# A selective scan on one core: GpSimd takes a coming tile's inputs ahead of two of its three products with C, and the sums over those products come one to two slots later

## The chip, the cores and the metric

The kernel runs on one core of a Trainium2 chip. The core's engines work side by side, each through its own queue in order: TensorE (PE in the profile, its weight loads PEld), VectorE (DVE), ScalarE (ACT), GpSimd (POOL) and SyncE (SP), which here issues all DMA transfers. They wait for each other through semaphores. The metric is the device time of one execution in microseconds.

## The reference, cut to what matters

A VSS-style block (layer norm, depthwise convolution, a selective scan in four directions, a gated norm, two convolutions with a channel gate) is followed by attention without softmax and a quantized feed-forward. The scan takes nearly all of the time:

```python
def _selective_scan(u, delta, A, Bs, Cs, D):      # 8 images, 4 directions, 192 channels, 4096 positions
    ...
    def step(hst, inp):
        u_i, dt_i, b_i, c_i = inp
        dA = jnp.exp(dt_i[..., None] * A)          # 16 states for each channel
        hst = dA * hst + (dt_i * u_i)[..., None] * b_i[:, :, None, :]
        y = jnp.einsum('bkdn,bkn->bkd', hst, c_i)
        return (hst, y)
    ...
    _, ys = lax.scan(step, h0, (u_t, dt_t, b_t, c_t))
    return ys.transpose(1, 2, 3, 0) + D[None, :, :, None] * u
```

## The kernel before, in words

The scan is cut into 256 *units*: 8 images, 4 directions (`order` 0 to 3) and 8 chunks of 512 positions. A unit has 192 channels times 16 states, that is 24 rows of work of 128 partitions by 512 positions. They are the 24 *slots* of a unit, in six tiles of four (`TILES`, `G` = 4): tile n has slots 4n to 4n + 3. Tiles 0 to 2 use the first half of B and C, tiles 3 to 5 the second.

What is done for one slot:

- ScalarE makes the decay, `da` = exp(delta * A) (L1111), into one of three PSUM banks, two slots ahead.
- GpSimd has made the inputs of the whole tile, `hb` = B * du, 128x2048, in `inputs` (L990). There are six `hb` buffers, so that a tile takes the buffer of the same tile of the unit before.
- VectorE scans (L1177). In a *banked* slot (`BANKED`: all of tiles 0, 2 and 4, and one or two slots of tile 5) the states go back into the PSUM bank and VectorE then multiplies them with C (L1179), and ScalarE copies the last state to `carry` (L1180) before the bank is used again. In the other slots the states go to `hb`, and ScalarE copies the carry of the whole tile once (L1185) after its last scan.
- For the slots that are not banked GpSimd multiplies with C, one instruction for a tile, in `outputs` (L996). A unit has three of these *lots*: tile 1 and tile 3 (128x2048) and what is left of tile 5 (128x1024 or 128x1536). It must follow the carry's copy, since it overwrites the states.
- TensorE adds up the states by products with a 0/1 matrix, in `sums` (L1016), in PSUM: tiles 0 and 1 together, tile 2, tiles 3 and 4 together, tile 5. After tile 5 it adds D * u or the sum so far (L1025), and ScalarE copies the result out in two pieces, `yt` (`gather`, L1035 in the transposed directions, L1038 in the others), which SP writes to HBM.

Beside it run the step sizes of the coming units (`step_sizes`: TensorE L955, ScalarE L963, L965 and L967, VectorE L969, GpSimd L972), their spread over partitions by DMA (`spread`, L984), the loads of B and C (`states`, L924), and two streams of *side work*: the front of the next image and the back end of the last one. A stream goes on by itself, a few instructions a slot: it issues a matmul group and its eviction (on ScalarE or VectorE) two slots later. `gated`, the first stage of the back end, takes a chunk once its y has been gathered.

The order of all queues is written out by hand. `plan` lists what is issued after the scan of each of the unit's 24 slots, and the main loop at the end of the function runs through the units and slots: first the carry copies left from the slot before, then the `da` of two slots on, the scan, its product with C, then the plan's list for the slot in the order in which it was put, then the side work. Each engine's queue is in that order; nothing is reordered afterwards. So what is put at an earlier slot stands further ahead in its engine's queue, and everything behind an instruction that waits, waits too.

Of the kernel before, what the change touches and what calls it, by code (L numbers as in the profile page):

```python
# [43 lines left out]
def kernel(ctx: ExitStack, tc: tile.TileContext, a, out):  # L44
# [689 lines left out]
    for b in range(out.shape[0]):  # L734
# [3 lines left out]
        for order, (pair, back) in enumerate((p, k) for p in s["pairs"] for k in range(2)):  # L738
            for i in range(NC):
                u = Unit()  # L740
# [305 lines left out]
    def plan(u, last, nxt, third):  # L1046

        at = [[] for _ in range(24)]

        def put(slot, f, *args):  # L1050
            at[slot].append((f, args))

        if last:
            put(0, outputs, last, 5)
            put(0, before, last)
            for m in range(2):
                put(m, sums, last, (3, 4), 2 + m)
            for m in range(2):
                put(5 + m, sums, last, (5,), m)
            put(7, states, u, 1, 1)  # L1060
            put(10, gather, last, 0)
            put(11, gather, last, 1)
        for n in range(6):
            to = (u, n + 2) if n < 4 else (nxt, n - 4)
            if to[0]:
                put(4 * n + 1, inputs, *to)
        if third and u.i % 2:
            put(16, step_sizes, (nxt, third), 5)
        put(8, outputs, u, 1)
        put(16, outputs, u, 3)  # L1070
        for m in range(4):
            put(13 + m, sums, u, (0, 1), m)
            if m < 2:
                put(18 + m, sums, u, (2,), m)
                put(22 + m, sums, u, (3, 4), m)
        if nxt:
            for i, slot in enumerate((0, 2, 4)):
                put(slot, step_sizes, (nxt,), i + 3)
            put(4, spread, nxt, 0, (0, 1))
            put(6, spread, nxt, 1, (0, 1))  # L1080
            put(10, states, nxt, 0, 0)
            put(15, states, nxt, 1, 0)
            put(20, states, nxt, 0, 1)
            if u.i % 2 == 0:
                put(15, spread, nxt, 0, (2,))
                put(16, spread, nxt, 1, (2,))
        if third:
            put(1, fetched_dt, third)
            put(9, fetched_u, third)
            for i, slot in enumerate((20, 22, 23)):  # L1090
                put(slot, step_sizes, (third,), i)
            if u.i % 2:
                for i, slot in enumerate((9, 11, 12, 13, 15)):
                    put(slot, step_sizes, (nxt, third), i)
                put(17, spread, nxt, 0, (2,))
                put(18, spread, nxt, 1, (2,))
            elif u.i + 3 < len(units):
                put(21, fetched_pair, third, units[u.i + 3])
        return at

    def at_index(i):
        return units[i] if 0 <= i < len(units) else None
# [39 lines left out]
    for u in units:  # L1142
        last, nxt, third = (at_index(u.i + d) for d in (-1, 1, 2))
# [19 lines left out]
        if u.start:  # L1163
            carry = sp.tile([P, 24], F32, tag="carry", name="carry")
        todo = plan(u, last, nxt, third)
        for slot in range(24):
            n, m = divmod(slot, G)
# [112 lines left out]
```

## Time and profile before

| | |
|---|---|
| runs | 11,218.44, 11,230.6 and 11,228.5 us; median 11,228.5 |
| profiled execution | 11,232.69 us, its span 11,230.9 us |
| scan loop, first scan to end of the last | 243.4 to 10,991.9 us |
| instructions of L1177, L996, L990 | 6,144, 768, 1,536 |
| mean of one, L1177 | 1.20 to 1.28 us by form |
| mean of one, L1179 | 0.69 us |
| one of L990 | 4.54 us |
| one of L996 | 4.53 us (128x2048), 3.45 (128x1536), 2.37 (128x1024) |
| one of L972, L1111, L1038 | 1.28, 0.69, 0.58 us |
| granted TensorE clock | 0.82 of full speed, mean |

Each line of the profile's groups gives a line of the kernel, the engine, what is written and read, the shape and the count; then the busy time in us and the mean of one in ns; and behind the bar the time that the engine sat idle just before these instructions, with what ended most of it. In the lists of waits a line reads: who waited, for whom, us in total, times, and the longest. In an order of time, the first two columns are the start and the duration in us, and brackets give the idle time before and its releaser.

### The profile page before, as it was taken

The page shows a single profiled execution, that of the slowest core. Times are in us where ns is not written, and L with a number is a line of the kernel's source. Part 1 is how long each engine was busy: PE and PEld are TensorE (multiplying, and loading weights), DVE is VectorE, ACT ScalarE, POOL GpSimd, SP SyncE. Part 2 cuts the span into 40 slices and gives each one's busy share as a digit, 9 for nine tenths or more (in the row PEclk, how much of TensorE's full clock was granted, in tenths as well). Part 3 has the DMA queues.
Part 4 walks back from the last instruction along what each step waited for, and adds up shares of the span by engine and source line. Part 5 has one row for each costly group of instructions (what it writes and reads, how often), then busy time and mean ns, then how long its engine had stood idle before and what let it go on. Part 6 is the DMA issues. An engine that isn't in the chain of part 4 may idle for free. (4 is left out here: it accounts for less than half of the span.)

```text
span 11230.9 us, 97011 instructions
## 1 busy us (share of the span) xinstructions
PE 8540.9 (76%) x23270; PEld 2316.7 (21%) x23270; DVE 10389.6 (93%) x10870; ACT 7480.8 (67%) x14898; POOL 10398.6 (93%) x2782
## 2 busy tenths in 40 slices
PE   7767668887788877887678876888767887676677
PEld 2111112221122211222112221222212221111212
DVE  1999999999999999999999999999999999999993
ACT  3666666667666676667766676676766667666674
POOL 1999999999999999999999999999999999999991
PEclk7887778887788877888788887888878888787778
DMA  4888888888888888888888888889888898888883
GB/s 108 203 194 206 190 196 211 213 219 199 200 211 217 207 197 213 204 216 214 192 215 205 215 218 196 203 210 226 202 202 212 208 223 199 193 196 199 201 200 91
DMA packets 1095376, 2253.25 MB, mean 201 GB/s; under 512 B 435993, under 2 KB 436698, under 8 KB 963731
## 3 DMA queue, kind: packets, MB, share of 16 engines
q1 hardware_dynamic: 1094803, 2247.05, 82.4%
q8 instruction: 184, 3.01, 0.1%
q14 instruction: 389, 3.19, 0.1%
HBM read 1507.14 MB, written 336.69 MB: 164 GB/s over the span
## 5 line engine op out<-in xcount | busy, mean ns | idle before, releaser
L990 POOL TENSOR_TENSOR hb<-b,du 128x2048 f32<-128x2048 f32 x1536 | 6938.9, 4535 | 9.0 <-PE p L1016 6.7
L1111 ACT ACTIVATE da<-delta,w_a_logs 128x512 f32<-128x512 f32 x6144 | 4216.9, 690 | 693.8 <-DVE hb L1177 573.0
L1016 PE MATMUL p<-hb,halves 128*64 128x512 f32 x12288 | 3813.7, 729 | 784.4 <-POOL hb L996 375.7
L1177 DVE TENSOR_TENSOR_SCAN da<-da,carry,hb 128x512 f32<-128x512 f32 x3087 | 3949.4, 1279 | 55.5 <-ACT da L1111 51.6
L996 POOL TENSOR_TENSOR hb<-hb,c 128x2048 f32<-128x2048 f32 (+2 forms) x768 | 2984.2, 3886 | 302.8 <-ACT carry L1185 250.2
L1177 DVE TENSOR_TENSOR_SCAN hb<-da,carry,hb 128x512 f32<-128x512 f32 x2289 | 2781.6, 1265 | 61.9 <-ACT da L1111 61.0
L1179 DVE TENSOR_TENSOR hb<-da,c 128x512 f32<-128x512 f32 x3528 | 2440.0, 692 | 155.5 <-DMA c<-xd 1.6
L1180 ACT COPY carry<-da 128x1 f32<-128x1 f32 x3528 | 554.9, 157 | 2335.1 <-DVE hb L1179 2325.2
L1016 PEld LDWEIGHTS p<-hb,halves 128*64 128x64 f32 x12288 | 913.0, 161 | 3512.6 <-issue 2112.9
L313 PE MATMUL conv<-f0im,taps 97*128 97x512 f32 (+1 forms) x2088 | 910.0, 669 | 92.2 <-ACT f0pre L369 52.1
L1177 DVE TENSOR_TENSOR_SCAN da<-da,hb 128x512 f32<-128x512 f32 x441 | 537.7, 1219 | 15.2 <-POOL hb L990 14.1
L972 POOL TENSOR_TENSOR ua<-nat,ua 128x512 f32<-128x512 f32 x256 | 327.4, 1279 | 228.6 <-DMA ub<-u 224.2
L955 PE MATMUL dt<-dts,dt_w 7*64 7x512 f32 (+1 forms) x1024 | 451.5, 661 | 12.7 <-DVE nat L969 10.9
L1025 PE MATMUL p<-u,ident 128*128 128x512 f32 x768 | 441.2, 703 | 4.3 <-DMA u<-y 3.9
L313 PEld LDWEIGHTS conv<-f0im,taps 97*128 97x128 f32 (+1 forms) x2088 | 255.6, 175 | 683.2 <-issue 527.6
L1177 DVE TENSOR_TENSOR_SCAN hb<-da,hb 128x512 f32<-128x512 f32 x327 | 377.8, 1203 | 4.9 <-ACT da L1111 4.9
L253 PE MATMUL ctr<-f1e,cen_c 96*96 96x512 f32 x402 | 229.4, 679 | 132.3 <-DVE f1e L648 93.8
L259 PE MATMUL var<-f1e,ones_c 96*96 96x512 f32 x350 | 207.9, 678 | 148.5 <-ACT f1e L256 135.4
L1185 ACT COPY carry<-hb 128x4 f32<-128x4 f32 (+2 forms) x768 | 147.0, 191 | 196.2 <-DVE hb L1177 183.8
L497 PE MATMUL cab<-f1im,cab_w 97*32 97x512 f32 x1044 | 267.2, 632 | 11.3 <-DMA f1im<-xld 7.6
L534 PE MATMUL cab<-f1m,cab_w 96*96 96x512 f32 x348 | 204.3, 714 | 93.3 <-ACT f1e L543 41.4
L967 ACT ACTIVATE nat<-nat,one 128x512 f32<-128x512 f32 x384 | 272.5, 710 | 0.1
(428 smaller groups left out, 7504.8 us busy)
## 6 DMA issues: line engine op xcount, KB each, us to landing
b<-xd SPq DMA_DIRECT2D x1024, 512.0 KB
c<-xd SPq DMA_DIRECT2D x1024, 512.0 KB
delta<-nat SPq DMA_DIRECT2D x1536, 128.0 KB
du<-ua SPq DMA_DIRECT2D x1024, 128.0 KB
y<-yt SPq DMA_DIRECT2D x512, 256.0 KB
u<-y SPq DMA_DIRECT2D x384, 256.0 KB
ua<-u SPq DMA_DIRECT2D x256, 256.0 KB
du<-ub SPq DMA_DIRECT2D x512, 128.0 KB
```

The lines of the kernel that those rows point to most:

```text
L313: nc.tensor.matmul(ps, taps[:, t, lo : lo + n], im[:, r0 + dy : r0 + dy + 8, dx : dx + HW], start=t == 0, stop=t == 8,)
L955: nc.tensor.matmul(ps, dt_w.rearrange("r j d -> r (j d)")[32 * w.k : 32 * w.k + R + 1, d], w.dts, start=True, stop=True)
L967: nc.scalar.activation(u.nat, u.nat, AF.Ln, bias=one)
L972: nc.gpsimd.tensor_tensor(x, u.nat, x, ALU.mult)
L990: nc.gpsimd.tensor_tensor(hb, u.bc[0, g], u.du[j].unsqueeze(1).to_broadcast([P, G, T]), ALU.mult)
L996: nc.gpsimd.tensor_tensor(hb, hb, u.bc[1, TILES[n][0]][:, lo:, :], ALU.mult)
L1016: nc.tensor.matmul(ps, halves, u.hb[n][:, i, :], start=TILES[n][0] == 0 and m == 0, stop=False, skip_group_check=True)
L1025: nc.tensor.matmul(ps, w, x, start=False, stop=True, skip_group_check=True)
L1111: nc.scalar.activation(da[q], u.delta[j], AF.Exp, scale=a_neg[:, u.k, j, g * G + m : g * G + m + 1])
L1177: nc.vector.tensor_tensor_scan(dd if banked else x, dd, x, 0.0 if u.start else col, ALU.mult, ALU.add)
L1179: nc.vector.tensor_tensor(hb[:, m, :], d, u.bc[1, g][:, m, :], ALU.mult)
L1180: kept.append(lambda col=col, d=d, at=first_at: nc.scalar.copy(col, d[:, at : at + 1]))
```

## The change

Within `plan`, three things move; every instruction stays.

- Inputs: before, the six `inputs` of a unit's list stood at slots 1, 5, 9, 13 (tiles 2 to 5 of this unit), 17 and 21 (tiles 0 and 1 of the next). Now tile 2's stands at slot 0 and tile 4's at slot 8.
- Products with C on GpSimd: that of the last unit's tile 5 goes from slot 0 to slot 1, that of tile 1 from slot 8 to slot 9. So each of the two now follows an input which it stood ahead of. The product of tile 3 stays at slot 16.
- Sums, and what hangs on them: over tiles 0 and 1 from slots 13 to 16 to slots 15 to 18, over tile 2 from 18 and 19 to 19 and 20, over the last unit's tile 5 (with L1025) from 5 and 6 to 7 and 8; `gather` from 10 and 11 to 11 and 12. Those over tiles 3 and 4 stay at 22, 23, 0 and 1.

```diff
         def put(slot, f, *args):
             at[slot].append((f, args))
 
+
+        for n, slot in enumerate((0, 5, 8, 13)):
+            put(slot, inputs, u, n + 2)
         if last:
-            put(0, outputs, last, 5)
+            put(1, outputs, last, 5)
             put(0, before, last)
             for m in range(2):
                 put(m, sums, last, (3, 4), 2 + m)
             for m in range(2):
-                put(5 + m, sums, last, (5,), m)
+                put(7 + m, sums, last, (5,), m)
             put(7, states, u, 1, 1)
-            put(10, gather, last, 0)
-            put(11, gather, last, 1)
-        for n in range(6):
-            to = (u, n + 2) if n < 4 else (nxt, n - 4)
-            if to[0]:
-                put(4 * n + 1, inputs, *to)
+            put(11, gather, last, 0)
+            put(12, gather, last, 1)
         if third and u.i % 2:
             put(16, step_sizes, (nxt, third), 5)
-        put(8, outputs, u, 1)
+        put(9, outputs, u, 1)
         put(16, outputs, u, 3)
+        if nxt:
+            put(17, inputs, nxt, 0)
+            put(21, inputs, nxt, 1)
         for m in range(4):
-            put(13 + m, sums, u, (0, 1), m)
+            put(15 + m, sums, u, (0, 1), m)
             if m < 2:
-                put(18 + m, sums, u, (2,), m)
+                put(19 + m, sums, u, (2,), m)
                 put(22 + m, sums, u, (3, 4), m)
```

## The prediction

> **What bounds the kernel now.** I read four views, in this order: the page's busy shares and groups, the waits of VectorE and GpSimd inside the scan loop (250 to 10990 us), then the order of time at two places.
>
> ```profile
> span 11230.9 us, 97011 instructions
> PE 8540.9 (76%) x23270; PEld 2316.7 (21%) x23270; DVE 10389.6 (93%) x10870; ACT 7480.8 (67%) x14898; POOL 10398.6 (93%) x2782
> DVE  1999999999999999999999999999999999999993
> ...
> L990 POOL TENSOR_TENSOR hb<-b,du 128x2048 f32<-128x2048 f32 x1536 | 6938.9, 4535 | 9.0 <-PE p L1016 6.7
> ...
> L996 POOL TENSOR_TENSOR hb<-hb,c 128x2048 f32<-128x2048 f32 (+2 forms) x768 | 2984.2, 3886 | 302.8 <-ACT carry L1185 250.2
> ```
>
> VectorE and GpSimd are both busy for 93%. The groups tell them apart only in part: GpSimd idles 303 us ahead of its products with C, mostly until ScalarE has copied the carry of the tile that VectorE just scanned. So which of the two waits for the other?
>
> ```profile
> DVE hb L1177 <- ACT da L1111: 65.8, 92, 3.0
> DVE da L1177 <- ACT da L1111: 51.6, 22, 5.8
> ...
> DVE da L1177 <- POOL hb L990: 6.5, 8, 1.9
> ```
>
> ```profile
> POOL hb L996 <- ACT carry L1185: 241.6, 207, 4.3
> ...
> POOL hb L990 <- PE p L1016: 6.7, 9, 1.0
> ```
>
> GpSimd waits for VectorE for 241.6 us, VectorE for GpSimd for 6.5 us. VectorE sets the pace. All its waits over 150 ns in the loop come to 273 us (212 for ScalarE, 54 for TensorE, 6.5 for GpSimd); the other idle time is some 43 ns between each scan and its product (152 us in 3,528). Hence the change can win at most 273 us, and only where it makes ScalarE's `da` or an eviction come earlier; GpSimd's own 242 us are worth nothing by themselves.
>
> The 273 us recur in the same slot of the same unit of each image. The largest (32.2 us in six images) is slot 11 of an image's unit 6:
>
> ```profile
> 1813.46 3.39 PE L1016 MATMUL p<-hb,halves 128*64 128x512 f32 x8
> 1814.32 4.51 POOL L996 TENSOR_TENSOR hb<-hb,c 128x2048 f32<-128x2048 f32 x1 [4.26 <-ACT carry L1185]
> ...
> 1818.83 1.96 PE L253 MATMUL ctr<-f1e,cen_c 96*96 96x512 f32 x4
> 1820.82 0.59 ACT L255 ACTIVATE f1e<-ctr 96x512 f32<-96x512 f32 x1 [5.99 <-PE ctr L253]
> ...
> 1822.71 1.29 DVE L1177 TENSOR_TENSOR_SCAN da<-da,carry,hb 128x512 f32<-128x512 f32 x1 [5.83 <-ACT da L1111]
> ```
>
> ScalarE stands at L255 for `ctr`, which queues on TensorE behind the last lot's sums (3.39 us) and L1025 (2.2 us); behind L255 stands the next `da`.
>
> The other place is tile 3 (slots 12 to 15), whose scans take 1.2 us a slot (slots with a product on VectorE take 1.93). ScalarE first, then VectorE:
>
> ```profile
> 2111.30 1.08 ACT L1035 COPY yt<-p 128x512 f32<-128x512 f32 x1
> 2112.41 0.16 ACT L1180 COPY carry<-da 128x1 f32<-128x1 f32 x1
> 2115.53 0.69 ACT L1111 ACTIVATE da<-delta,w_a_logs 128x512 f32<-128x512 f32 x1 [2.96 <-DVE hb L1177]
> 2116.15 1.10 ACT L1035 COPY yt<-p 128x512 f32<-128x512 f32 x1
> ```
>
> ```profile
> 2114.22 1.28 DVE L1177 TENSOR_TENSOR_SCAN hb<-da,carry,hb 128x512 f32<-128x512 f32 x1
> 2116.25 1.28 DVE L1177 TENSOR_TENSOR_SCAN hb<-da,carry,hb 128x512 f32<-128x512 f32 x1 [0.76 <-ACT da L1111]
> ```
>
> This `da` was given the PSUM bank that the scan at 2114.22 still reads, so it waits for that scan and the next scan waits for it. Slots 13 to 16 hold 24.4, 25.7, 10.9 and 5.9 us of the waits.
>
> **The change part by part.** Nothing is added or removed: of 1,536 inputs (L990) 512 are recorded a slot earlier, of 768 products with C 511 a slot later; of the 6,144 matmuls of the sums 3,068 go two slots later and 1,024 one; 510 of 512 at L1025 two later; 510 of the 512 `yt` copies one later, with their `y` writes on SP; and 13 chunks of `gated`, which wait for `y`, one later.
>
> *GpSimd's order.* The input of tile 4 (4.54 us, slot 8) runs in front of the product of tile 1, that of tile 2 (slot 0) in front of the last unit's tile 5 product. The waits ahead of just these two products sum to 105 and 118 us; they go, since the input has nothing to wait for. Behind the pair GpSimd's queue is the same, so the later tile 3 product, `ua` and SP's `du` transfers come no later. The two products end up to 4.5 us later; the sums over them are two slots (3.2 to 3.9 us) later. The `c` transfer of slot 15 waits for the tile 1 product: its issue now follows that product by a median 3.7 us, so it slips by about 1 us, with some nine slots (15 us) to its first use. VectorE's worth: at most the 6.5 us.
>
> A wait arises instead. The six `hb` buffers rotate, so the next unit's first input (slot 17) needs the sums over tile 0, recorded in slots 15 to 18 instead of 13 to 16. The built program has it wait for the matmul of slot 18. GpSimd now comes there a median 5.3 us after that matmul. Two slots take 3.9 us of it, and the product before it can come up to 1 us sooner. Setting the two against each other unit by unit, this input waits 75 us in all (if TensorE reaches the sums as early as it now reaches tile 2's in slot 18) to 220 us (if it lags behind its slot as it now does in slot 16). The input is ready a median 3.5 us before its scan, so VectorE loses 0 to 14 us of that. Against the 6.5 us I take 0 for the whole part.
>
> *ScalarE's tile 3.* Two things, of opposite sign. In the built programs a `da` takes the bank of the scan just before it 40 times before (35 of them in slot 13) and 5 times after (none in slot 13). In those 35 units VectorE waits 24.0 us in slot 13 and 18.8 in slot 14: −43 us at best, 0 if ScalarE is late there for other reasons. I take −38, as the other units show next to no wait in slot 13. Against it, the second `yt` copy (0.58 us at L1038, 1.09 at L1035) moves from slot 11, of 1.93 us, to slot 12, of 1.2 us, in front of the `da` of slots 15 and 16. In odd units, where ScalarE also does L965 and L967 there, that `da` is ready a median 0.41 us before its scan (even units 1.23). Summing copy minus lead over the units where that is positive gives 53 us (40 in odd units); 0 if the lead grows by what slot 13 loses. I take +42. Together +4, bounds −43 and +53.
>
> *Side work on TensorE.* In unit 6, TensorE's new order is two sums, `ctr`, two sums, L1025: 1.7 + 2.2 = 3.9 us less in front of `ctr`. Its chain, with `gated`, starts up to one slot (1.9 us) later, so 2.0 to 3.9 of the 5.8 us go, in six images: −12 to −23, taken −18. In unit 17 `gram` (L612, 2.4 us in four images) likewise has two sums and L1025 behind it instead of in front: −5 (0 to −10). In unit 1 L462 and L463 come into the slot of L1025 instead of the one behind it, where VectorE's L465 already waits 2 us: up to a slot more in seven images, +8 (0 to +13). The remaining 170 us of waits are collisions whose sides shift by one or two slots; matmuls of sums recorded in the same or the previous slot ahead of a side group count 4,112 before and 4,174 after: a redraw, 0, with ±30.
>
> *The clock.* The longest spells of slots without sums are now 2 to 4 and 7 to 12; they become 2 to 6 and 9 to 14. The granted clock, averaged by slot, is 0.73 to 0.77 in slots 11 to 14, behind the long spell, and 0.92 to 0.95 in slots 17 and 18. I take +5 us for evictions from a colder TensorE in slots 5 to 8, between 0 and +20 (a tenth more on the some 200 us that hang on TensorE or ScalarE).
> The Trainium skill, TensorE: Matmul & The Clock Gate (What's actually happening), says that the clock halves after an idle window of about 3.4 us. The trace agrees in kind: at 1807.85 two records of L356 take 2.02 us, at 1813.46 eight of L1016 take 3.39. By the rule alone the spell of slots 2 to 6 (2 x 1.93 + 3 x 1.2 = 7.5 us) would leave TensorE cold in every unit with little side work, so that the first two sums of slot 7 take some 1.7 us more; on a handful of evictions in seven images that is an estimated +12 us, and the sum would be some 7 us higher.
>
> *Sum:* 0 + 4 − 18 − 5 + 8 + 5 = −6 us on 11,232.7 (the span 11,230.9 and 1.8 around it), 11,226.7. The median of the runs shown, 11,228.5, lies 4.2 below the profiled execution, so I say 11,223.
>
> **The rivals.**
> 1. *Slower: the `yt` copy in the fast tile decides.* If banks free late anyway and the copy's 53 us stand almost whole, with the clock's and the redraw's share: +25 to +80, some 11,275. For: leads of 0.1 us in a quarter of the odd units. Against: the 35 reuses are gone from the program. It decides where ScalarE's lead in slot 15 is below 0.58 us.
> 2. *Faster: freed banks and freed `ctr`.* −43 and −23 come whole, the copy costs half (26): −40, with the redraw −25 to −70, some 11,180.
> 3. *GpSimd is the real bound* and its 223 us come back as time: 11,005. Against: VectorE waits 6.5 us for it.
> 4. *The change does nothing on GpSimd*, the wait only moving to the buffer (up to 220 us): this lies inside the forecast, as both waits are off VectorE's path.
>
> **How the numbers follow.** About 0.2% (22 us) is what a measurement of this kernel can tell from no change. The forecast (within 22 us of before) has 0.40, rival 1 0.30, rival 2 0.28, rival 3 0.02. So faster 0.30, same 0.40, slower 0.30; the forecast's own range is 11,206 to 11,251. To leave out no more than 2 in 10 the range reaches into both sides: 11,170 to 11,285.
>
> **What would show it.** Right: GpSimd's wait for the carry falls from 242 us to under 100, mostly at tile 3's product, while L990 waits 75 to 220 us for L1016; VectorE's waits in slot 13 nearly vanish, those in slots 15 and 16 grow to 40 to 60 us; slot 11 of unit 6 loses 2 to 4 us; VectorE's waits sum to 250 to 290 us. Wrong: VectorE waiting tens of us for L990 (the buffer), new waits over 3 us for TensorE in slots 17 to 20, or longer scans and products (1.27 and 0.69 us).

## The result and the profile after

The changed kernel takes 11,190.7 us (median of 6 runs, 11,184.5 to 11,200.1), the kernel before 11,231.6 us (6 runs). The ratio is 0.9966 with a 95% interval from 0.9956 to 0.9977: faster by 0.34%, about 41 us. The profiled execution took 11,185.26 us with a span of 11,183.5, which is 47.4 us less than the span before.

`plan` has two lines more now, so that L1111, L1177, L1179, L1180 and L1185 of before are L1113, L1179, L1181, L1182 and L1187. From the page of the changed kernel, the busy times and the two groups of GpSimd:

```profile
span 11183.5 us, 97037 instructions
PE 8542.6 (76%) x23270; PEld 2324.5 (21%) x23270; DVE 10381.2 (93%) x10870; ACT 7484.3 (67%) x14898; POOL 10391.8 (93%) x2782
...
L990 POOL TENSOR_TENSOR hb<-b,du 128x2048 f32<-128x2048 f32 x1536 | 6935.2, 4545 | 116.1 <-PE p L1016 93.2
...
L996 POOL TENSOR_TENSOR hb<-hb,c 128x2048 f32<-128x2048 f32 (+2 forms) x768 | 2994.5, 3899 | 74.1 <-ACT carry L1187 65.7
```

The products with C wait 74 us where they waited 303, and the inputs 116 where they waited 9. The waits of GpSimd and of VectorE in the loop (250 to 10,950 us):

```profile
POOL ub L972 <- DVE nat L969: 123.2, 55, 6.1
POOL hb L990 <- PE p L1016: 93.2, 51, 5.6
POOL hb L996 <- ACT carry L1187: 65.7, 50, 9.5
```

```profile
DVE hb L1179 <- ACT da L1113: 51.5, 77, 2.4
DVE da L1179 <- ACT da L1113: 31.4, 27, 3.2
...
DVE da L1179 <- POOL hb L990: 9.8, 11, 1.3
```

GpSimd's wait for the carry fell from 242 us to 66 (9.5 of them stand behind the last scan), but GpSimd now stands 93 us ahead of its inputs, until TensorE has summed the old contents of the buffer, and 123 ahead of `ub`, until VectorE has run L969. All its waits in the loop went from 363 to 329 us, and its share of busy time is the same. VectorE's waits for `da` fell from 117 us to 83.

Where did the 47.4 us come from? Start and tail of the span gave 3.5 us. In the loop VectorE's waits over 150 ns, the wait ahead of the first scan among them, fell from 283.1 to 245.2 us, its busy time by 8.3, and its gaps under 150 ns grew by 2. Scans and products last as long as before (1.27 and 0.69 us). Sorted by place, beside the terms of the prediction (us):

| where VectorE spends it | before | after | change | predicted |
|---|---|---|---|---|
| waits of the scans in slots 13 and 14 | 50.1 | 7.3 | −42.8 | −38 |
| waits of the scans in slots 15 and 16 | 18.7 | 46.1 | +27.4 | +42 |
| slot 11 of unit 6 | 32.2 | 9.3 | −22.9 | −18 |
| L465 in unit 1 | 13.5 | 2.7 | −10.8 | +8 |
| `gram` (L614) in unit 17 | 10.6 | 2.0 | −8.6 | −5 |
| slot 0, for the inputs of tile 0 | 8.6 | 17.7 | +9.1 | 0 |
| all other waits (redraw, clock) | 149.4 | 160.1 | +10.7 | +5 |
| busy: L572, eight instructions | 17.6 | 9.1 | −8.5 | no term |

Of the 18.7 us in slots 15 and 16, 6.0 were waits for GpSimd's inputs in slot 16, and these went. The waits for `da` alone, which the prediction's +42 priced, grew by 33 us, from 12.7 to 45.6.

Unit 6 is read in the timeline of the changed kernel (TensorE's sums, the side work, then ScalarE and VectorE):

```profile
1799.48 1.08 PE L1016 MATMUL p<-hb,halves 128*64 128x512 f32 x4
...
1801.54 1.96 PE L253 MATMUL ctr<-f1e,cen_c 96*96 96x512 f32 x4 [0.98 <-DVE f1e L465]
...
1803.42 1.08 PE L1016 MATMUL p<-hb,halves 128*64 128x512 f32 x4
...
1804.43 1.12 PE L1025 MATMUL p<-u,dd_a 128*128 128x512 f32 x2
...
1805.44 0.57 ACT L255 ACTIVATE f1e<-ctr 96x512 f32<-96x512 f32 x1
...
1806.42 1.28 DVE L1179 TENSOR_TENSOR_SCAN da<-da,carry,hb 128x512 f32<-128x512 f32 x1
```

`ctr` runs between the two halves of the sums and ahead of L1025. When ScalarE comes to L255, `ctr` is ready, and the scan has no wait in brackets, where it waited 5.83 us before. This is the first of the six images; in the five others 1.8 to 1.9 us of the wait are left, which are the 9.3 us of the table.

### The profile page after: what moved, and what is told of

Same layout as the page of the kernel before. It is cut to its first block, busy times and chain, and to the rows that moved or that the text cites. A ratio compares the mean times of both kernels' runs of the same rounds, so it can differ in the third digit from the quotient of the medians.

```text
span 11183.5 us, 97037 instructions
## 1 busy us (share of the span) xinstructions
PE 8542.6 (76%) x23270; PEld 2324.5 (21%) x23270; DVE 10381.2 (93%) x10870; ACT 7484.3 (67%) x14898; POOL 10391.8 (93%) x2782
## 5 line engine op out<-in xcount | busy, mean ns | idle before, releaser
L990 POOL TENSOR_TENSOR hb<-b,du 128x2048 f32<-128x2048 f32 x1536 | 6935.2, 4545 | 116.1 <-PE p L1016 93.2
L1113 ACT ACTIVATE da<-delta,w_a_logs 128x512 f32<-128x512 f32 x6144 | 4219.3, 690 | 572.2 <-DVE hb L1179 451.9
L1016 PE MATMUL p<-hb,halves 128*64 128x512 f32 x12288 | 3845.1, 715 | 817.0 <-POOL hb L996 601.8
L1179 DVE TENSOR_TENSOR_SCAN da<-da,carry,hb 128x512 f32<-128x512 f32 x3087 | 3949.0, 1279 | 42.9 <-ACT da L1113 31.4
L1179 DVE TENSOR_TENSOR_SCAN hb<-da,carry,hb 128x512 f32<-128x512 f32 x2289 | 2783.1, 1265 | 44.6 <-ACT da L1113 42.3
L1181 DVE TENSOR_TENSOR hb<-da,c 128x512 f32<-128x512 f32 x3528 | 2440.5, 692 | 157.7 <-DMA c<-xd 1.5
L1182 ACT COPY carry<-da 128x1 f32<-128x1 f32 x3528 | 554.1, 157 | 2463.7 <-DVE hb L1181 2453.1
L1016 PEld LDWEIGHTS p<-hb,halves 128*64 128x64 f32 x12288 | 930.0, 158 | 3552.4 <-issue 2090.0
L313 PE MATMUL conv<-f0im,taps 97*128 97x512 f32 (+1 forms) x2088 | 880.0, 648 | 45.2 <-ACT f0pre L369 20.5
L972 POOL TENSOR_TENSOR ua<-nat,ua 128x512 f32<-128x512 f32 x256 | 330.0, 1289 | 239.1 <-DVE nat L969 234.8
L1179 DVE TENSOR_TENSOR_SCAN da<-da,hb 128x512 f32<-128x512 f32 x441 | 537.4, 1219 | 10.7 <-POOL hb L990 9.6
L1025 PE MATMUL p<-u,ident 128*128 128x512 f32 x768 | 458.0, 726 | 0.0
L1179 DVE TENSOR_TENSOR_SCAN hb<-da,hb 128x512 f32<-128x512 f32 x327 | 378.1, 1204 | 9.2 <-ACT da L1113 9.2
L972 POOL TENSOR_TENSOR ub<-nat,ub 128x512 f32<-128x512 f32 x128 | 165.0, 1289 | 132.9 <-DVE nat L969 126.6
L969 DVE SCALAR_TENSOR_TENSOR nat<-dt,nat 128x512 f32<-128x512 f32 x384 | 259.5, 676 | 9.7 <-ACT nat L967 9.7
```

The source lines that it names most:

```text
L313: nc.tensor.matmul(ps, taps[:, t, lo : lo + n], im[:, r0 + dy : r0 + dy + 8, dx : dx + HW], start=t == 0, stop=t == 8,)
L972: nc.gpsimd.tensor_tensor(x, u.nat, x, ALU.mult)
L990: nc.gpsimd.tensor_tensor(hb, u.bc[0, g], u.du[j].unsqueeze(1).to_broadcast([P, G, T]), ALU.mult)
L1016: nc.tensor.matmul(ps, halves, u.hb[n][:, i, :], start=TILES[n][0] == 0 and m == 0, stop=False, skip_group_check=True)
L1025: nc.tensor.matmul(ps, w, x, start=False, stop=True, skip_group_check=True)
L1113: nc.scalar.activation(da[q], u.delta[j], AF.Exp, scale=a_neg[:, u.k, j, g * G + m : g * G + m + 1])
```

## The experiments

Two theories stood at first. A: the gain is in VectorE's waits for ScalarE and TensorE (banks of tile 3, side work), and GpSimd's freed wait is worth nothing. B: GpSimd's freed wait makes it. The expectations below name them so.

**The order on GpSimd alone.** The kernel before with the new places of inputs and products; sums and `gather` as before.

```diff
+        for n, slot in enumerate((0, 5, 8, 13)):
+            put(slot, inputs, u, n + 2)
...
-            put(0, outputs, last, 5)
+            put(1, outputs, last, 5)
...
-        put(8, outputs, u, 1)
+        put(9, outputs, u, 1)
```

> Only GpSimd's order of the change (inputs of tiles 2 and 4 ahead of the products of tiles 5 and 1); sums and gathers as before. Theory A (VectorE's waits for ScalarE and TensorE make the gain; GpSimd's waits are worth nothing): GpSimd's waits for the carry fall from 242 to under 100 us and the time stays within 0.2% of before, or grows by up to 0.5%, since the sums over tiles 0 and 1 (slot 13) now wait on TensorE for a product that ends up to 4.5 us later; VectorE's waits in slots 13 and 14 stay at some 45 to 50 us. Theory B (GpSimd's freed 220 us make the gain): faster by 0.3 to 0.4%, as the whole change.

It took 11,241.3 us, a ratio of 1.0016 [1.0007, 1.0025]: slightly slower. Its waits of GpSimd and of VectorE (one line was added, so the copy is L1186, the scan L1178):

```profile
POOL ub L972 <- DVE nat L969: 156.0, 75, 5.6
POOL hb L996 <- ACT carry L1186: 143.8, 75, 8.3
```

```profile
DVE hb L1178 <- ACT da L1112: 63.1, 90, 1.4
DVE da L1178 <- ACT da L1112: 47.0, 22, 6.4
```

Some 98 us less of waiting for the carry (241.6 to 143.8, where under 100 had been expected) brought nothing. The wait moved on: for `nat`, ahead of L972, it grew from 61 to 177 us, and all of GpSimd's waits in the loop went from 363 to 379. VectorE's waits for `da` are as before (110 against 117 us), and all its waits are 299.9 us (283.1 before); those of L450, an instruction of the side work, grew from 47 to 78, and the cause of this stays open. Theory B falls: the new order on GpSimd alone gains no time, and the next run has most of the gain without it.

**Sums and gather alone.** GpSimd's order as before, the sums and `gather` at their new slots.

```diff
-                put(5 + m, sums, last, (5,), m)
+                put(7 + m, sums, last, (5,), m)
...
-            put(10, gather, last, 0)
-            put(11, gather, last, 1)
+            put(11, gather, last, 0)
+            put(12, gather, last, 1)
...
-            put(13 + m, sums, u, (0, 1), m)
+            put(15 + m, sums, u, (0, 1), m)
             if m < 2:
-                put(18 + m, sums, u, (2,), m)
+                put(19 + m, sums, u, (2,), m)
```

> Only the later sums and gathers; GpSimd's order as before. Theory A: nearly the whole gain, faster by 0.25 to 0.45%; VectorE's waits in slot 13 under 2 us, in slot 15 some 40 us, slot 11 of unit 6 some 10 us; GpSimd still waits 200 us or more for the carry. Theory B: within 0.15% of before.

11,197.6 us, 0.9973 [0.9963, 0.9984]: most of the gain. VectorE's waits are 245.3 us, the same as in the changed kernel, with slots 13 and 14 at 0 and 7.4 and slot 11 of unit 6 at 9.5.

```profile
POOL hb L996 <- ACT carry L1185: 144.3, 130, 3.9
POOL hb L990 <- PE p L1016: 111.0, 55, 7.3
```

One part of what was expected failed: GpSimd's wait for the carry fell although its order is that of before. The later sums hold up the inputs (111 us ahead of L990), GpSimd comes later to its products, and the carry is there. The two waits are one slack of GpSimd, which is spent at one instruction or the other.

**The gather alone.** Only the two `gather` lines of the diff above.

> Only the two gathers one slot later (11 and 12). The built program then has 5 reuses of a PSUM bank by the da right behind its scan, none in slot 13 (before 40 and 35). Theory A: VectorE's wait in slot 13 falls from 24 us to under 2, that in slot 14 from 26 to about 8, that in slot 15 grows from 11 to 40 (the yt copy); slot 11 of unit 6 keeps its 32 us; together within 0.2% of before, at most 0.25% faster. If instead the sums alone make the gain: no change of the waits in slots 13 to 15.

11,212.3 us, 0.9991 [0.9982, 0.9999]. Slot 13 lost all its waits and slot 14 half (24.4 and 25.7 to 0 and 12.3 us), slots 15 and 16 grew from 18.7 to 45.8, and slot 11 of unit 6 stayed at 29.0. So the two `yt` copies alone change how the banks fall: in the built program a `da` takes the bank of the scan just before it 5 times, none of them in slot 13, as in the changed kernel. Why the pool's choice, which is made when the program is built, falls so was not looked into.

**Banks in a fixed turn.** If the bank matters and not the copy, giving each `da` its bank by number should do the same and more.

```diff
-    BANKS = {"da": 3, "dt": 1, "f0": 1, "f1": 1, "y01": 1, "y2": 1}
+    BANKS = {"da0": 1, "da1": 1, "da2": 1, "dt": 1, "f0": 1, "f1": 1, "y01": 1, "y2": 1}
...
-        da[q] = bank("da", "da")
+        da[q] = bank(f"da{q % 3}", "da")
```

> Kernel before, with the three PSUM banks of da taken strictly in turn (no reuse at distance one or two). Theory A: the waits of VectorE in slots 13 and 14 fall from 50 us to under 12, slot 15 stays near 11: faster by 0.3 to 0.4%. Rival (those waits come from ScalarE's load, not from the bank): the waits only move to slots 14 to 16 and the time is within 0.15% of before.

The kernel before with these two lines: 11,168.6 us, 0.9949 [0.9937, 0.9961], more than the 0.3 to 0.4% that had been expected. By the medians it is ahead of the change (0.9966), though the intervals just overlap. VectorE's waits fell to 228.3 us: slots 13 to 16 hold 28.6 in place of 68.8, while slot 11 of unit 6 keeps its 35.6.

> Kernel after, with the three PSUM banks of da taken strictly in turn. Theory A (the change's gain is partly that the reuse at distance one is gone, partly the later sums): what the banks gained in the kernel before (0.51%) is here partly had already, so 0.15 to 0.4% faster than after, 0.5 to 0.75% faster than before; VectorE's wait in slot 15 (40 us, the yt copy in slot 12 behind a da that waits for the scan of slot 12) falls to under 20. If the 40 us are the copy's alone, they stay over 30 us and the kernel gains under 0.1% over after.

The changed kernel with them: 11,147.4 us, 0.9931 [0.9918, 0.9943]. Slot 15 fell from 40.4 to 18.3 us, so half of what the moved copy seemed to cost there was banks as well.

**Gather put back in the changed kernel.** The changed kernel with `gather` at slots 10 and 11, with the program's own choice of banks and with fixed ones.

> Kernel after with the two gathers at slots 10 and 11 as before. The built program then has 65 reuses of the bank just scanned, 60 in slot 13. Theory A: VectorE's waits in slots 13 and 14 come back and exceed those of before (60 instead of 35 units at 0.7 + 0.55 us: 60 to 80 us), slot 15 falls to about 11 us; slot 11 of unit 6 stays at 10 us or less; in all 0.1 to 0.4% slower than after, within 0.25% of before. If the reuse does not matter: as fast as after or faster, since the yt copy is out of the fast slot.

11,231.5 us, 1.0005 [0.9996, 1.0013]: the whole gain is gone. Here a `da` takes the bank just scanned 65 times, 60 of them in slot 13, and slots 13 and 14 hold 46.3 and 32.7 us.

```profile
DVE hb L1179 <- ACT da L1113: 102.4, 144, 2.3
DVE da L1179 <- ACT da L1113: 32.5, 24, 3.1
```

The first of these two lines was 51.5 us, 77 times, in the changed kernel.

> Kernel after with the gathers at slots 10 and 11 and the banks of da strictly in turn: later sums and GpSimd's new order, with no yt copy in the fast tile and no reuse. Theory A: slots 13 to 16 together under 30 us, slot 11 of unit 6 under 10 us: 0.6 to 0.85% faster than before, the fastest of all. If ScalarE's load in slots 10 to 13 is what makes the waits: no faster than the kernel before with fixed banks (0.51%).

11,151.9 us, 0.9934 [0.992, 0.9947], against 11,147.4 with the copies at the new slots. With the banks fixed, the slot of the copy makes no difference that can be told: slots 13 to 16 hold 34 us with the old slots (under 30 had been expected, and the fastest time of all, which it is not) and 30 with the new. The same edit that cost some 40 us with the program's own choice costs nothing that can be told here, and so those 40 us were banks.

**Which of the sums.** On fixed banks, with GpSimd's order and `gather` as before: only the sums over tile 5 two slots later (`put(7 + m, sums, last, (5,), m)`), and then all three groups of sums later.

> Kernel before with fixed banks and only the sums over the last unit's tile 5 (with L1025) two slots later, so that in unit 6 ctr stands in front of them on TensorE. Against the kernel before with fixed banks: theory A: slot 11 of unit 6 falls from 35.6 us to under 12, 0.1 to 0.3% faster than it (0.6 to 0.8% faster than before). If that wait is ScalarE's own: no change there, and 0.51% as with fixed banks alone.

11,141.6 us (11,133 to 11,158), 0.9926 [0.9914, 0.9939]. Slot 11 of unit 6 fell from 35.6 to 11.1 us by this one line.

> Kernel before with fixed banks and all three groups of sums at the change's slots (15 to 18, 19 and 20, 7 and 8); GpSimd's order and the gathers as before. Theory A: only the tile 5 sums matter (ctr), the others are a redraw: within 0.15% of the run with the tile 5 sums alone and fixed banks (0.9926). If the sums over tiles 0 to 2 carry a gain of their own: 0.15% or more faster than that.

11,163.6 us (11,154 to 11,173), 0.9946 [0.9934, 0.9959]. The later sums over tiles 0 to 2 bring nothing: unit 6 is at 9.3 us, and GpSimd waits 66.7 us for TensorE ahead of L990, which it does not with tile 5's sums alone. Whether they cost something stays open: the medians say 22 us, the intervals just overlap, and of the profiled executions this one is the shorter (span 11,152.5 against 11,156.6).

**L572.** Behind the 8.5 us of busy time stands one line of the side work, eight instructions of VectorE with 96x96 elements. From the timeline, an image of the kernel before, then the same image of the changed one:

```profile
2241.25 9.01 POOL L990 TENSOR_TENSOR hb<-b,du 128x2048 f32<-128x2048 f32 x2
...
2247.83 2.49 DVE L572 TENSOR_SCALAR dgate<-ident,gate 96x96 f32<-96x96 f32 x1
```

```profile
2231.16 4.53 POOL L990 TENSOR_TENSOR hb<-b,du 128x2048 f32<-128x2048 f32 x1
...
2234.29 0.16 DVE L571 RECIPROCAL gate<-gate 96x1 f32<-96x1 f32 x1
...
2234.49 1.26 DVE L572 TENSOR_SCALAR dgate<-ident,gate 96x96 f32<-96x96 f32 x1
```

In seven images L572 ends 0.06 to 0.07 us after the GpSimd instruction that runs beside it (2250.26 and 2235.69 here), however long it has then taken. In the last image GpSimd is idle, and it takes 0.267 us. The shorter stay comes from GpSimd's order: the eight instructions take 9.1 us with that order alone and 18.5 with the later sums and `gather` alone. The kernel before was run with the same work on ScalarE:

```diff
-            nc.vector.tensor_scalar(dgate, ident[:C, :C], gate, None, ALU.mult)
+            nc.scalar.activation(dgate, ident[:C, :C], AF.Identity, scale=gate)
```

> Kernel before, with the scaling of the 96x96 identity by the gate (L572) done by ScalarE instead of VectorE. L572 takes 2.48 us in seven images, each time until 0.06 us after the end of an L990 on GpSimd, and 0.27 us in the last image, where GpSimd is idle. If it waits for GpSimd (a shared way into SBUF), VectorE is spared 7 x 2.4 = 17 us, less what ScalarE's wait for the reciprocal costs its next da: 0.05 to 0.15% faster, ScalarE's instruction 0.2 to 0.3 us. If the 2.48 us are the instruction's own, ScalarE takes as long and the time is the same.

11,210.2 us, 0.9989 [0.998, 0.9998]. The line's own view gives minimum, median and maximum in ns:

```profile
L572 ACT ACTIVATE dgate<-ident,gate x8: 374/374/375, 2242.9 to 11090.5; 96x96 f32<-96x96 f32 x8
```

On ScalarE each takes 0.374 us beside the same instructions of GpSimd, and VectorE's busy time in the loop fell by 17.1 us, nearly the 17.6 of L572.

**The three together.** Fixed banks, tile 5's sums two slots later, L572 on ScalarE; GpSimd's order and `gather` as before.

> Kernel before with fixed banks, the tile 5 sums two slots later and L572 on ScalarE: the parts that paid, without GpSimd's new order. If they add up: 0.8 to 0.95% faster than before; if the waits only move on, no faster than the run with the tile 5 sums alone and fixed banks (0.74%).

11,126.0 us (11,115.9 to 11,128.0), 0.9912 [0.9899, 0.9926]: 0.88% faster than before, where the change gave 0.34%.

```profile
DVE hb L1177 <- ACT da L1111: 37.5, 34, 2.2
...
DVE da L1177 <- ACT da L1111: 25.3, 16, 3.1
```

```profile
POOL hb L996 <- ACT carry L1185: 189.7, 180, 7.8
```

The fastest kernel of the study has 63 us of waits for `da` on VectorE, where the kernel before had 117, and 190 us of GpSimd's wait for the carry (7.8 of them behind the last scan), which the change set out from.

## Why the prediction was right and where it was wrong

The forecast was no change within 22 us, its own range 11,206 to 11,251; the time came out below that, inside the range given for all cases. What came true is rival 2, freed banks and freed `ctr`, put at 11,180 with a chance of 0.28. The sum itself (−6 us) missed the profiled difference by 41 us; the range held because rival 2 had been priced into it.

- **What bounds the kernel: right.** VectorE sets the pace. GpSimd's order alone took 98 us from its wait for the carry and was 0.16% slower, and fixed banks gained 0.51% with GpSimd's order as before. Rivals 3 and 4 are answered with it: no 223 us came back, and the wait did move to the buffer (93 us, foreseen as 75 to 220). The prediction did not see the second place it moved to, `nat` of L969 (61 to 137 us over the whole loop).
- **GpSimd's order worth 0, bounds to +14: near in the waits, with a term missing.** Slot 0 lost 9.1 us, nearly all in waits for tile 0's inputs (9.8 us in eleven units, beside the wait ahead of the first scan of all; 3.9 with the later sums alone, 1.8 with GpSimd's order alone). Against it the 6.0 us of waits for inputs in slot 16 went. What the order did bring is not in its waits: L572, below.
- **Banks of tile 3: right.** The 35 reuses were priced at −38, with −43 at best; it was −42.8. Putting `gather` back brought such reuses back (60 in slot 13), and fixing the banks removed the waits without the change.
- **The `yt` copy: the term that decided the forecast, and mis-sized.** It was +42; slots 15 and 16 together grew by 27.4 us, their waits for `da` by 33. The step that failed priced the copy against ScalarE's lead alone, and counted only `da` that take the bank of the scan just before. By copy minus lead 114 units should wait 53 us in all; in 51 of these, with 15 of the 53 us, the changed kernel has no wait in slots 15 and 16. And banks stand beside the copy. It follows the `da` of slot 14, which in the built program of the changed kernel takes the bank of slot 12's scan, two slots before, in 138 of 256 units; 35.3 of slot 15's 40.4 us fall in these. With fixed banks there is no such reuse, slot 15 has 18.3 us, and the copy's slot makes no difference that can be told in the time. Unit 104 is one of the 138:

```profile
4585.00 3.44 DVE L1179 TENSOR_TENSOR_SCAN hb<-da,hb 128x512 f32<-128x512 f32 x3
...
4586.24 0.69 ACT L1113 ACTIVATE da<-delta,w_a_logs 128x512 f32<-128x512 f32 x1 [0.97 <-DVE hb L1179]
...
4586.87 0.58 ACT L1038 COPY yt<-p 128x512 f32<-128x512 f32 x1
...
4587.54 0.69 ACT L246 ACTIVATE f1e<-var,eps 96x512 f32<-96x512 f32 x1
...
4589.49 1.22 DVE L1179 TENSOR_TENSOR_SCAN hb<-da,hb 128x512 f32<-128x512 f32 x1 [1.05 <-ACT da L1113]
```

  ScalarE loses 0.97 us until the first of the three scans has freed a bank, then 0.58 to the copy, then more to side work (L246 and the instruction behind it); together they come to a wait of 1.05 us at the scan of slot 15. No run takes the side work's share by itself.
- **Side work: `ctr` and `gram` right, a little small** (−22.9 and −8.6 for −18 and −5). **L465 of unit 1 had the wrong sign.** The prediction put L462 and L463 into the slot of L1025 and so behind it. The timeline shows them between the two halves of the sums, as `ctr` is in unit 6, with L1025 after them. The kernel before, then the changed one:

```profile
2943.35 3.35 PE L1016 MATMUL p<-hb,halves 128*64 128x512 f32 x8
...
2947.68 1.07 PE L1025 MATMUL p<-u,dd_b 64*64 64x512 f32 x2
...
2948.68 1.10 PE L462 MATMUL attn<-f1x,wy_a 128*96 128x512 f32 x2
...
2950.84 0.69 DVE L465 TENSOR_TENSOR f1e<-attn,f1e 96x512 f32<-96x512 f32 x1 [2.18 <-PE attn L463]
```

```profile
2926.18 1.97 PE L1016 MATMUL p<-hb,halves 128*64 128x512 f32 x4
...
2928.09 1.92 PE L462 MATMUL attn<-f1x,wy_a 128*96 128x512 f32 x2
...
2929.93 1.10 PE L463 MATMUL attn<-f1pre,wy_b 64*96 64x512 f32 x2
...
2930.96 1.08 PE L1016 MATMUL p<-hb,halves 128*64 128x512 f32 x4
...
2931.41 0.68 DVE L465 TENSOR_TENSOR f1e<-attn,f1e 96x512 f32<-96x512 f32 x1
...
2931.97 0.70 PE L1025 MATMUL p<-u,dd_a 128*128 128x512 f32 x1
```

  In this image the wait went, and two of the seven keep 1.5 and 1.2 us: −10.8 us where +8 was forecast. This is 19 us of the 41 between the forecast's sum (−6) and the profiled difference (−47); slots 15 and 16 are 15 of them, and L572 8.5.
- **Redraw 0 ± 30 and clock +5: together +11, but not a redraw.** The largest in it are L465 in unit 7, 0 to 14.9 us, and L476 in unit 6, 3.4 to 12.4. Both come with the sums over tile 5: with fixed banks, moving these alone takes them from 0 to 13.7 and from 3.4 to 14.4. In unit 7 L462 and L463 now run behind both halves of the sums and L1025 in all seven images, and L465 waits 2 us for them. So the collision that the prediction priced at +8 does occur, in unit 7 and not in unit 1; over the two units VectorE waits 4 us more at L465. That this lies near the forecast's +8 is luck.
- **The clock: right in its place, wrong in its mean.** The mean went up, 0.824 to 0.830. By slots, the granted clock was 0.80 to 0.82 in slots 5 to 8 and is now 0.67 to 0.70; in slots 21 to 23 it was 0.78 to 0.81 and is now 0.90 to 0.92. The prediction put the change down to the moved sums, but GpSimd's order alone, with the sums at their old slots, already gives 0.70 in slot 5 (0.81 again in slot 7), 0.86 to 0.88 in slots 21 to 23 and a mean of 0.836; the later sums and `gather` alone give 0.72 to 0.73 in slots 5 to 8, 0.86 to 0.90 in slots 21 to 23 and 0.826. The sums in the colder slots became some 12% slower (a record of L1016 takes 0.80 us on average in slots 5 to 7 before, 0.90 in slots 6 to 8 after). VectorE's waits for TensorE fell all the same, from 54 to 42 us. What the prediction cited from the Trainium skill, TensorE: Matmul & The Clock Gate (What's actually happening), agrees with the colder slots (0.67 to 0.70); the 12 us that were estimated from it cannot be told apart from the other shifts here.
- **L572: not seen at all.** Its 17.6 us stood in the busy time of VectorE, which the prediction took as fixed, and 8.5 of them went, through GpSimd's order.

## What to carry to other kernels

Waiting time is worth something only on the engine that sets the pace; 242 us of GpSimd's waiting were worth nothing here, and the fastest kernel still has most of them. Where a pool chooses a buffer when the program is built, read from the built program which one each tile got: moving a copy by one slot moved some 40 us, and a fixed turn of three banks gave 0.51% by itself, where the whole change gave 0.34%. When work is moved in a shared queue, write out the order instruction by instruction for every unit with side work, since the same move that freed `ctr` freed L463 in unit 1, which the forecast had going the other way, and held it up in unit 7.

## What the runs showed of the hardware that had not been expected

An instruction of VectorE of 0.267 us took up to 2.49 us beside GpSimd in the kernel before: L572 scales a 96x96 tile in SBUF by a column, and ends 0.06 to 0.07 us after the L990 that runs when it is issued, in seven images of eight. Other short ones beside the same L990 keep their length (L571, 0.16 us beside it in both kernels), and on ScalarE the work of L572 takes 0.374 us. The Trainium skill, SBUF — State Buffer (Who interferes with whom), gives the reason: VectorE and GpSimd have a pair of ports in common, a `tensor_scalar` of VectorE can use it in its two-port modes, and whoever comes first holds it for the whole instruction. The trace agrees in each of the seven images; that L572 ran in such a mode is not shown by itself.
